# A channel mix contracted in two 64-deep halves instead of one 128-deep product

## The chip, the core and the metric

The kernel runs on one core of one Trainium2 chip. The metric is the device time of one execution in microseconds (us). A core has several engines with queues of their own: TensorE (PE; its weight loads are shown apart, as PEld) multiplies matrices into PSUM, VectorE (DVE), ScalarE (ACT) and GpSimd (POOL) work element by element, SyncE (SP) issues most of the transfers. Each engine works its queue in order; a semaphore makes an instruction wait for another engine.

## The reference

The input is x, 4 images of 64 channels of 256 by 256, in 32-bit floats. Four layers follow each other. Layers 0, 1 and 3 are long convolutions with a separable causal filter that a small network generates, each plus `x * bias`. Layer 2, which the change concerns, is a channel mix in the Haar domain with a soft threshold:

```python
f1 = haar2d(x)
acc = jnp.zeros_like(f1[:, :conv_w.shape[1]])
for i in range(v.shape[0]):                                   # two parts
    f3 = f1 * v[i]
    f4 = jnp.einsum('bchw,oc->bohw', f3, conv_w[i])
    f5 = jnp.sign(f4) * jax.nn.relu(jnp.abs(f4) - tau[i])
    acc = acc + f5
y = haar2d(acc, inverse=True)
return y + x
```

v and tau hold one value for each coefficient and part, the same for all channels; conv_w is 2 matrices of 64 by 64.

## The kernel before

The filters are made once, in the first 55 us, and written to DRAM. Then the four images are worked one after the other, each in three phases.

Phase A runs over the 64 channels. A convolution is two products with triangular matrices (lines 139 and 140), the data being the stationary operand; two convolutions are followed by a Haar transform down the columns (L197), and ScalarE copies the result into two large SBUF tiles z, one for each half of the columns, laid out as partition, row, channel. Phase C runs over the channels again: the inverse Haar transform (L286, L297), the residual, and the last convolution.

Phase B lies between them, runs over 64 groups of four rows of coefficients, and transfers nothing. A group is worked in two steps. `b_rows`: TensorE transforms along the rows (L227, product pg; two rows of 64 channels fill the 128 columns of a stationary operand, so the result has row r of the pair and channel c on partition 64 r + c), ScalarE copies it to f (L235), and three small VectorE operations of two elements mend the border coefficients (L238, L239, L240). `b_mix`: TensorE contracts the channels (L248, product px), VectorE scales by v (L258), ScalarE takes Abs into mag (L262) and Sign in place (L263), GpSimd subtracts tau (L264), VectorE clamps at 0 and multiplies by the sign (L265), and two GpSimd additions, one for each half of the columns, sum the two parts into z (L268).

Line 248 contracts 128 partitions although a row has 64 channels: the moving operand wb holds the mixing matrix twice, for row 0 in its upper 64 rows and first 128 columns, for row 1 in its lower 64 rows and last 128 columns, and zeros elsewhere. So one product of 256 columns gives both rows:

```python
wb = const.tile([P, 2, P], F32, name="wb")
nc.vector.memset(wb, 0.0)
for r in range(2):
    nc.sync.dma_start(wb[r * C : (r + 1) * C, r, :], wmix)
```

A product of 32-bit floats is carried out as two matmul instructions, each with a weight load of its own.

The order on the engines' queues is not that of the program text. The framework schedules the instructions by their dependencies and by its own estimate of their durations, so a changed instruction can move others on every engine. Pools set how far it can run ahead: f has 3 buffers, f4 and mag 2 each, px 2 (of two PSUM banks), pg and the other products 4. VectorE's butterfly on rows 0 and 128 of z stands before and after phase B.

Of the kernel before, what the change touches and what calls it, by code (L numbers as in the profile page):

```python
# [9 lines left out]
F32 = mybir.dt.float32  # L10
AF = mybir.ActivationFunctionType
ALU = mybir.AluOpType
PSUM = bass.MemoryType.PSUM
DRAM = bass.MemoryType.DRAM

B, C, S, EMB, ORD = 4, 64, 256, 33, 64
P = 128
# [1 line left out]

INV_2PI = float(np.float32(1.0 / (2.0 * math.pi)))  # L20
MAGIC = float(1.5 * 2.0**23)
# 2 pi in three parts, of which the first two give exact products with small integers
C1 = 6.28125
C2 = 2028.0 / 2.0**20
C3 = float(np.float32(2.0 * math.pi - C1 - C2))
# [6 lines left out]

@with_exitstack
def conv_seq_kernel(ctx, tc, x, fz, fw, bias, decay, haar, haar_inv, vt, taut, wmix, out):
    """Three separable causal long convolutions with a Haar-domain channel mix between the second and the third.

    The 2-D FFT convolution with k = hx (x) hy on a doubled grid is Tx X Ty^T / 512 with lower triangular
    Toeplitz Tx, Ty. A product with the data as the stationary operand contracts its partition axis and swaps
    the axes, so two of them give back the layout they started from. The filters are kept from the last value to
    the first: their Toeplitz matrices are then overlapping rows in DRAM, read back to front by the products.  # L40

    A Haar transform of 256 points is two local ones of 128 points whose sums are then added and subtracted;
    coefficients are kept in that order (block, local index), in which v and tau are laid out too.
    """
    nc = tc.nc

    const = ctx.enter_context(tc.tile_pool(name="const", bufs=1))
    dram = ctx.enter_context(tc.tile_pool(name="dram", bufs=1, space=DRAM))

# [1 line left out]
    hbt = const.tile([P, P], F32, name="hbt")  # L51
    hb = const.tile([P, P], F32, name="hb")
    hinv = const.tile([P, 2, S], F32, name="hinv")
    nc.sync.dma_start(hbt, haar[0])
    nc.sync.dma_start(hb, haar[1])
    nc.sync.dma_start(hinv, haar_inv)
    wb = const.tile([P, 2, P], F32, name="wb")
    nc.vector.memset(wb, 0.0)
    for r in range(2):
        nc.sync.dma_start(wb[r * C : (r + 1) * C, r, :], wmix)  # L60
    vsb = const.tile([P, S // 4, 16], F32, name="vsb")
    tsb = const.tile([P, S // 4, 16], F32, name="tsb")
    nc.scalar.dma_start(vsb, vt)
# [1 line left out]
    bsb = const.tile([P, 3, C], F32, name="bsb")  # L65
    nc.sync.dma_start(bsb, ap(bias, 0, [[0, P], [C, 3], [1, C]]))

# [1 line left out]
    pads = [dram.tile([C, 2, ROW], F32, name=f"pad{layer}") for layer in range(3)]  # L69
    with tc.tile_pool(name="filt", bufs=2) as fp, tc.tile_pool(name="fps", bufs=4, space=PSUM) as fps:  # L70
        dsb = fp.tile([C, S], F32, name="dsb", bufs=1)
        nc.sync.dma_start(dsb, decay)
        zs, ws = [], []
        for layer in range(3):
            z = fp.tile([EMB, S + 2 * ORD], F32, name=f"z{layer}", tag="z", bufs=3)
            nc.sync.dma_start(z, fz[layer])
            w = fp.tile([ORD, 2, 3 * ORD + 4], F32, name=f"w{layer}", tag="w", bufs=3)
            nc.sync.dma_start(w, fw[layer])
            zs.append(z)
            ws.append(w)  # L80
        cur = {}
        both = [(layer, axis) for layer in range(3) for axis in range(2)]
        for step in range(3):
            for layer, axis in both:
                z, w = zs[layer], ws[layer]
                ps = fps.tile([ORD, S], F32, name=f"fp{step}_{layer}_{axis}", tag="fps")
                if step == 0:
                    nc.tensor.matmul(ps, z[:, S + axis * ORD : S + (axis + 1) * ORD], z[:, :S], start=True, stop=True)
                else:
                    nc.tensor.matmul(  # L90
                        ps, w[:, axis, (step - 1) * ORD : step * ORD], cur[layer, axis], start=True, stop=True
                    )
                par = 3 * ORD
                u = fp.tile([ORD, S], F32, name=f"u{step}_{layer}_{axis}", tag="u", bufs=3)
                nc.vector.tensor_scalar(
                    u, ps, w[:, axis, par + step : par + step + 1], w[:, axis, par + 3 : par + 4], ALU.add, ALU.mult
                )
                # into [-pi, pi], where the Sin table is defined
                k = fp.tile([ORD, S], F32, name=f"k{step}_{layer}_{axis}", tag="k", bufs=3)
                nc.vector.tensor_scalar(k, u, INV_2PI, MAGIC, ALU.mult, ALU.add)  # L100
                nc.vector.tensor_scalar(k, k, -MAGIC, None, ALU.add)
                for c in (C1, C2, C3):
                    nc.vector.scalar_tensor_tensor(u, k, -c, u, ALU.mult, ALU.add)
                nc.vector.tensor_scalar(u, u, PI_IN, -PI_IN, ALU.min, ALU.max)
                h = fp.tile([ORD, S], F32, name=f"h{step}_{layer}_{axis}", tag="h", bufs=12)
                nc.scalar.activation(h, u, AF.Sin)
                cur[layer, axis] = h
        for layer, axis in both:
            w = ws[layer]
            ps = fps.tile([C, S], F32, name=f"fo_{layer}_{axis}", tag="fps")  # L110
            nc.tensor.matmul(ps, w[:, axis, 2 * ORD : 3 * ORD], cur[layer, axis], start=True, stop=True)
            f = fp.tile([C, ROW], F32, name=f"f_{layer}_{axis}", tag="f")
            nc.vector.memset(f[:, S:], 0.0)
            nc.vector.scalar_tensor_tensor(  # L114
                f[:, :S], ps, 1.0 / (2 * S) if axis == 0 else 1.0, dsb, ALU.mult, ALU.mult
            )
            nc.sync.dma_start(pads[layer][:, axis, :], f)

# [1 line left out]
    zpool = ctx.enter_context(tc.tile_pool(name="zpool", bufs=1))  # L120
    tp = ctx.enter_context(tc.tile_pool(name="toep", bufs=7))
    io = ctx.enter_context(tc.tile_pool(name="io", bufs=3))
# [2 lines left out]
    psx = ctx.enter_context(tc.tile_pool(name="psx", bufs=2, space=PSUM))  # L125

    def toeplitz(layer, c, name):
        """[p, k, m] = h_k[S - 1 - m - p], 0 where that is negative, for the filters down (0) and along (1)"""
        t = tp.tile([P, 2, S], F32, name=name, tag="toep")
        nc.sync.dma_start(t, ap(pads[layer], c * 2 * ROW, [[1, P], [ROW, 2], [1, S]]))  # L130
        return t
# [2 lines left out]
        return psm.tile([P, 2, S], F32, name=name, tag="mm")  # L134

    def contract(ps, src, t):
        """ps[:, m, :] = (the m-th half of src's free axis) x (causal filter of src's partition axis)"""
        for m in range(2):
            nc.tensor.matmul(ps[:, m, :], src[:, 0, m * P : (m + 1) * P], t[:, ::-1], start=True, stop=False)  # L139
            nc.tensor.matmul(ps[:, m, P:], src[:, 1, m * P : (m + 1) * P], t[:, : P - 1 : -1], start=False, stop=True)  # L140
# [5 lines left out]
                    stages[s](tick - s)  # L146

    def butterfly(z):
        """rows 0 and P of z: their sum and their difference"""
        d = mx.tile([P, C], F32, name="bfly", tag="bfly")  # L150
        nc.vector.tensor_sub(d, z[:, 0, :], z[:, P, :])
        nc.vector.tensor_add(z[:, 0, :], z[:, 0, :], z[:, P, :])
# [2 lines left out]
    for b in range(B):  # L155
        keep = dram.tile([C, P, 2, S], F32, name=f"keep{b}")
        z = [zpool.tile([P, S, C], F32, name=f"z{h}_{b}", tag=f"z{h}") for h in range(2)]

# [1 line left out]
        st = {}  # L160

        def a_load(c):
# [53 lines left out]
        for h in range(2):  # L216
            butterfly(z[h])

# [1 line left out]
        mixed = {}  # L220

        def b_rows(g):
# [19 lines left out]

        def b_mix(g):
            f = mixed.pop(g)
            ps = psx.tile([P, 2, 2, S], F32, name=f"px_{b}_{g}", tag="mix")
            for q in range(2):
                for h in range(2):
                    nc.tensor.matmul(  # L248
                        ps[:, h, q, :],
                        f[:, q, h * P : (h + 1) * P],  # L250
                        wb.rearrange("p r n -> p (r n)"),
                        start=True,
                        stop=True,
                    )
            scale = vsb[:, g, :].unsqueeze(2).to_broadcast([P, 16, C])
            shrink = tsb[:, g, :].unsqueeze(2).to_broadcast([P, 16, C])
            f4 = mx.tile([P, 16, C], F32, name=f"f4_{b}_{g}", tag="f4")
            nc.vector.tensor_tensor(  # L258
                f4, ps.rearrange("p h q (r i o) -> p (h q r i) o", r=2, i=2), scale, ALU.mult
            )  # L260
            mag = mx.tile([P, 16, C], F32, name=f"mag_{b}_{g}", tag="mag")
            nc.scalar.activation(mag, f4, AF.Abs)  # L262
            nc.scalar.activation(f4, f4, AF.Sign)  # L263
            nc.gpsimd.tensor_tensor(mag, mag, shrink, ALU.subtract)  # L264
            nc.vector.scalar_tensor_tensor(mag, mag, 0.0, f4, ALU.max, ALU.mult)  # L265
            parts = mag.rearrange("p (h r i) o -> p h r i o", h=2, i=2)
            for h in range(2):
                nc.gpsimd.tensor_tensor(  # L268
                    z[h][:, 4 * g : 4 * g + 4, :], parts[:, h, :, 0, :], parts[:, h, :, 1, :], ALU.add
                )  # L270

        pipelined(S // 4, [b_rows, b_mix])
        for h in range(2):
            butterfly(z[h])

# [1 line left out]
        def c_load(c):  # L277
            r = io.tile([P, 2, S], F32, name=f"r_{b}_{c}", tag="in", bufs=4)
            nc.sync.dma_start(r, keep[c])
# [36 lines left out]


def _haar_order():
    """the place in the reference's order of the coefficient (block, local index)"""
    at = np.zeros((2, P), np.int64)  # L320
    for q in range(2):
        at[q, 0] = q
        n = 1
# [4 lines left out]


def _haar_local():  # L330
    """rows: the 128-point Haar functions, the constant one divided by sqrt(2)"""
    h = np.zeros((P, P))
    h[0] = 1.0 / 16.0
    n = 1
# [76 lines left out]
```

## Time and profile before

| What | us |
|---|---|
| Median of 3 runs (4255.77 to 4256.11) | 4256.06 |
| Span of the profiled execution | 4252.5 |
| TensorE products px, L248, 2048 instructions | 598.1 |
| TensorE products pg, L227, 2048 instructions | 291.8 |
| GpSimd subtractions, L264, 256 of 2.002 | 512.0 |
| GpSimd additions, L268, 512 of 0.946 | 471.9 |
| VectorE clamp and multiply, L265, 256 of 1.634 | 418.2 |
| VectorE scale, L258, 256 of 1.216 | 310.7 |
| VectorE small operations, L238 to L240, 768 | 400.0 |
| ScalarE Abs and Sign, L262 and L263, 512 | 541.1 |

The span runs from the first to the last instruction of the profiled execution; the median is of whole executions and stands 3.6 us above it. Busy times of groups on the same engine overlap where instructions are pipelined, on TensorE above all, so they can't simply be added there. In a line of instructions the columns are the line of the kernel, the engine, the operation, what is written and read, and the shapes; "128*128" ahead of a shape gives rows and columns of the stationary operand. In a timeline the first two columns are the start and the duration, "x2" says that two instructions were merged into one line, and the brackets give idle time before it and what ended it. Where a line or tile is asked for by itself, its durations stand as least, median and greatest in ns, and the list below gives idle microseconds and how many times.

### The profile page before, as it was taken

What the parts mean: (1) busy time and instruction counts of PE and PEld (TensorE: products, weight loads), DVE (VectorE), ACT (ScalarE), POOL (GpSimd) and SP (SyncE); (2) the same over time, 40 slices, a digit from 0 to 9 for tenths busy, and PEclk for the clock granted to TensorE, in tenths of its full rate; (3) what the DMA queues carried; (4) which work ended last, traced back from release to release, by engine and by line L of the source; (5) the groups of instructions that cost most, each with busy time, mean ns of one, the idle gap of its engine ahead of it and who ended that gap; (6) DMA issues with size and microseconds to landing.
All of it is one profiled execution on the core that took longest, in us unless ns stands there. A gap on an engine that the chain in (4) does not pass through costs nothing.

```text
span 4252.5 us, 56979 instructions
## 1 busy us (share of the span) xinstructions
PE 3805.2 (89%) x21552; PEld 3445.5 (81%) x21552; DVE 1864.7 (44%) x2491; ACT 1531.2 (36%) x2323; POOL 975.2 (23%) x772
## 2 busy tenths in 40 slices
PE   7999876899999977699999997769999999676999
PEld 5999655799999965589999995559999998555998
DVE  4222788322222288822222228972222223886222
ACT  2333555222233355522233335542223333554222
POOL 0000588100000068800000007870000000776000
PEclk9999989899999998899999999889999999988999
DMA  4566100355555600045556650005555665000554
GB/s 127 171 172 173 45 1 1 109 149 152 164 171 172 173 21 1 1 131 150 151 168 172 172 169 1 1 3 149 151 150 170 172 173 144 1 1 22 152 151 124
DMA packets 424114, 476.23 MB, mean 112 GB/s; under 512 B 28993, under 2 KB 357924, under 8 KB 423844
## 3 DMA queue, kind: packets, MB, share of 16 engines
q1 hardware_dynamic: 317060, 337.29, 29.7%
q10 hardware_dynamic: 106784, 135.30, 8.7%
q8 instruction: 174, 2.85, 0.3%
q14 instruction: 96, 0.79, 0.1%
HBM read 337.67 MB, written 134.81 MB: 111 GB/s over the span
## 4 chain that ended last, share of the span: by engine, by line
PE 72%; POOL 11%; DVE 10%; issue 4%; ACT 3%; DMA 0%; SPq 0%; POOLq 0%; DVEq 0%; ACTq 0%
PE py L139 16%; PE pa L139 16%; PE pw L286 11%; PE pa L140 8%; PE py L140 8%; POOL mag L264 6%; PE pz L197 5%; PE pu L297 5%; POOL z L268 5%; DVE mag L265 5%; PE px L248 2%; DVE f L258 2%; ACT mag L262 1%; PE pg L227 1%; DVE f L239 1%
## 5 line engine op out<-in xcount | busy, mean ns | idle before, releaser
L264 POOL TENSOR_TENSOR mag<-mag,tsb 128x1024 f32<-128x1024 f32 x256 | 512.0, 2002 | 2856.4 <-ACT mag L262 2775.4
L173 ACT COPY a<-pa 128x512 f32<-128x512 f32 x768 | 450.3, 586 | 1470.7 <-PE pa L140 1470.7
L139 PE MATMUL py<-t,a 128*128 128x256 f32 x3072 | 918.5, 381 | 5.9 <-ACT a L173 5.9
L248 PE MATMUL px<-wb,f 128*128 128x256 f32 x2048 | 598.1, 438 | 363.2 <-DVE f L239 147.9
L248 PEld LDWEIGHTS px<-wb,f 128*128 128x128 f32 x2048 | 412.9, 216 | 492.3 <-issue 133.7
L140 PEld LDWEIGHTS py<-t,a 128*128 128x128 f32 x3072 | 583.7, 190 | 78.9
L140 PE MATMUL py<-t,a 128*128 128x128 f32 x3072 | 590.1, 274 | 0.0
L286 PE MATMUL pw<-hinv,z 128*128 128x256 f32 x2048 | 502.0, 388 | 33.1 <-POOL z L268 33.1
L286 PEld LDWEIGHTS pw<-hinv,z 128*128 128x128 f32 x2048 | 474.9, 302 | 46.0 <-POOL z L268 36.6
L139 PEld LDWEIGHTS py<-t,a 128*128 128x128 f32 x3072 | 486.3, 192 | 15.3 <-ACT a L173 8.8
L186 DVE SCALAR_TENSOR_TENSOR y<-y,bsb,py 128x512 f32<-128x512 f32 x256 | 191.5, 748 | 699.8 <-PE py L140 695.0
L268 POOL TENSOR_TENSOR z<-mag 128x256 f32<-128x256 f32 x512 | 471.9, 946 | 77.0 <-DVE mag L265 30.5
L265 DVE SCALAR_TENSOR_TENSOR mag<-mag,f 128x1024 f32<-128x1024 f32 x256 | 418.2, 1634 | 144.2 <-POOL mag L264 141.1
L186 DVE SCALAR_TENSOR_TENSOR y<-u,bsb,py 128x512 f32<-128x512 f32 x256 | 191.3, 747 | 604.2 <-PE py L140 594.7
L262 ACT ACTIVATE mag<-f 128x1024 f32<-128x1024 f32 x256 | 270.3, 1056 | 504.7 <-POOL z L268 313.5
L186 DVE SCALAR_TENSOR_TENSOR y<-x,bsb,py 128x512 f32<-128x512 f32 x256 | 191.3, 747 | 490.8 <-PE py L140 490.8
L299 DVE TENSOR_TENSOR u<-pu,r 128x512 f32<-128x512 f32 x256 | 177.1, 692 | 394.8 <-PE pu L297 394.8
L290 ACT COPY w<-pw 128x512 f32<-128x512 f32 x256 | 150.0, 586 | 547.5 <-PE pw L286 547.5
L258 DVE TENSOR_TENSOR f<-px,vsb 128x1024 f32<-128x1024 f32 x256 | 310.7, 1216 | 12.2 <-PE px L248 8.9
L139 PE MATMUL pa<-t,x 128*128 128x256 f32 x1024 | 306.9, 382 | 4.8 <-DVE f L114 4.8
L227 PEld LDWEIGHTS pg<-hbt,z 128*128 128x128 f32 x2048 | 292.2, 212 | 20.7 <-ACT z L201 6.0
L139 PE MATMUL pa<-t,y 128*128 128x256 f32 x1024 | 305.8, 380 | 0.0
(44 smaller groups left out, 4393.6 us busy)
## 6 DMA issues: line engine op xcount, KB each, us to landing
t<-pad SPq DMA_DIRECT2D x768, 256.0 KB, 3.5
x<-in_x SPq DMA_DIRECT2D x256, 256.0 KB, 3.7
keep<-y ACTq DMA_DIRECT2D x256, 256.0 KB, 3.3
r<-keep SPq DMA_DIRECT2D x256, 256.0 KB, 2.6
out_y<-y ACTq DMA_DIRECT2D x256, 256.0 KB, 3.3
pad<-f SPq DMA_DIRECT2D x6, 96.0 KB, 2.7
vsb<-in_vt ACTq DMA_DIRECT2D x1, 512.0 KB, 4.0
tsb<-in_taut ACTq DMA_DIRECT2D x1, 512.0 KB, 5.1
```

The lines of the kernel that those rows point to most:

```text
L139: nc.tensor.matmul(ps[:, m, :], src[:, 0, m * P : (m + 1) * P], t[:, ::-1], start=True, stop=False)
L140: nc.tensor.matmul(ps[:, m, P:], src[:, 1, m * P : (m + 1) * P], t[:, : P - 1 : -1], start=False, stop=True)
L173: nc.scalar.copy(a, ps)
L186: nc.vector.scalar_tensor_tensor(y, s[res], bsb[:, layer, c : c + 1], ps, ALU.mult, ALU.add)
L227: nc.tensor.matmul(ps[:, q, h * P : (h + 1) * P], z[h][:, r : r + 2, :].rearrange("p r c -> p (r c)"), hbt, start=True, stop=True,)
L248: nc.tensor.matmul(ps[:, h, q, :], f[:, q, h * P : (h + 1) * P], wb.rearrange("p r n -> p (r n)"), start=True, stop=True,)
L258: nc.vector.tensor_tensor(f4, ps.rearrange("p h q (r i o) -> p (h q r i) o", r=2, i=2), scale, ALU.mult)
L262: nc.scalar.activation(mag, f4, AF.Abs)
L264: nc.gpsimd.tensor_tensor(mag, mag, shrink, ALU.subtract)
L265: nc.vector.scalar_tensor_tensor(mag, mag, 0.0, f4, ALU.max, ALU.mult)
L268: nc.gpsimd.tensor_tensor(z[h][:, 4 * g : 4 * g + 4, :], parts[:, h, :, 0, :], parts[:, h, :, 1, :], ALU.add)
L286: nc.tensor.matmul(ps[:, m, :], z[h][:, m * P : (m + 1) * P, c], hinv[:, h, :], start=(h == 0), stop=(h == 1))
```

## The change

wb shrinks to one copy of the mixing matrix on each half of the partitions, without zeros. Each product of 128 partitions by 256 columns becomes two of 64 partitions by 128 columns, one for each row of the pair, whose operands lie on partitions 0 to 63 and 64 to 127. The row r becomes the outermost axis of px[...]. The axes that follow (those of v and tau, prepared on the host, and of mag in the additions) are reordered to match; the additions write rows 0, 2, 1, 3 of the group.

```diff
-    wb = const.tile([P, 2, P], F32, name="wb")
-    nc.vector.memset(wb, 0.0)
+    wb = const.tile([P, P], F32, name="wb")
     for r in range(2):
-        nc.sync.dma_start(wb[r * C : (r + 1) * C, r, :], wmix)
+        nc.sync.dma_start(wb[r * C : (r + 1) * C, :], wmix)
...
-            ps = psx.tile([P, 2, 2, S], F32, name=f"px_{b}_{g}", tag="mix")
-            for q in range(2):
-                for h in range(2):
-                    nc.tensor.matmul(
-                        ps[:, h, q, :],
-                        f[:, q, h * P : (h + 1) * P],
-                        wb.rearrange("p r n -> p (r n)"),
-                        start=True,
-                        stop=True,
-                    )
+            ps = psx.tile([P, 2, 2, 2, P], F32, name=f"px_{b}_{g}", tag="mix")
+            for h in range(2):
+                for q in range(2):
+                    for r in range(2):
+                        on = slice(r * C, (r + 1) * C)
+                        nc.tensor.matmul(
+                            ps[:, r, h, q, :], f[on, q, h * P : (h + 1) * P], wb[on, :], start=True, stop=True
+                        )
...
-                f4, ps.rearrange("p h q (r i o) -> p (h q r i) o", r=2, i=2), scale, ALU.mult
+                f4, ps.rearrange("p r h q (i o) -> p (r h q i) o", i=2), scale, ALU.mult
...
-            parts = mag.rearrange("p (h r i) o -> p h r i o", h=2, i=2)
+            parts = mag.rearrange("p (r h q i) o -> p r h q i o", r=2, h=2, q=2)
             for h in range(2):
                 nc.gpsimd.tensor_tensor(
-                    z[h][:, 4 * g : 4 * g + 4, :], parts[:, h, :, 0, :], parts[:, h, :, 1, :], ALU.add
+                    z[h][:, 4 * g : 4 * g + 4, :].rearrange("p (q r) o -> p r q o", q=2),
+                    parts[:, :, h, :, 0, :],
+                    parts[:, :, h, :, 1, :],
+                    ALU.add,
                 )
...
-        return lay(a.reshape(2, S // 4, 4, 2, P).transpose(4, 1, 3, 2, 0).reshape(P, S // 4, 16))
+        return lay(a.reshape(2, S // 4, 2, 2, 2, P).transpose(5, 1, 3, 4, 2, 0).reshape(P, S // 4, 16))
```

The rest of the diff drops comments, which shifts line numbers: in the changed kernel the product px is L251, the scale L257, Abs and Sign L261 and L262, the subtraction L263, the clamp L264 and the addition L267.

## The prediction

> **What bounds the kernel now.** I read the busy table first, then the granted clock and busy time in the four stretches of the channel mix, then who waits for the lines that the change touches, and last the timeline of GpSimd and VectorE inside one stretch.
>
> ```profile
> PE 3805.2 (89%) x21552; PEld 3445.5 (81%) x21552; DVE 1864.7 (44%) x2491; ACT 1531.2 (36%) x2323; POOL 975.2 (23%) x772
> ...
> 60.00:452.00 392.00, 389.98 (x2543) 363.53 (x2541) 95.88 (x131) 140.79 (x255) 0.00 (x0) 1.00 0.61 173
> 452.00:765.00 313.00, 214.53 (x1031) 176.90 (x1032) 266.49 (x330) 163.87 (x192) 245.27 (x192) 0.87 0.00 1
> ```
>
> Columns of the last two lines: stretch, length, busy time of PE, PEld, DVE, ACT, POOL, clock, DMA share, GB/s. TensorE's 89% is an average over different stages. Phase A of the first image (60 to 452) fills TensorE: 390 of 392 us. Phase B (452 to 765), the only stage that the change touches, has it busy for 215 of 313 us, while VectorE is busy for 266 and GpSimd for 245. The other three images' phase B are within 4 us of these figures. So in phase B TensorE is not the engine to relieve; who waits for its product says the same:
>
> ```profile
> L258 DVE TENSOR_TENSOR f<-px,vsb x256: 1208/1212/1226, 456.6 to 3901.7; 128x1024 f32<-128x1024 f32 x128
> ...
>   ACT f L235: 22.3, 14
>   DVE f L258: 8.9, 14
> ```
>
> The product px (L248) is read by L258. VectorE stood idle for it for 8.9 us in the whole run, and ScalarE's copies (L235), queued on TensorE behind it, for 22.3 us. The chain of waits gives px 2% (85 us), but that is where the chain happens to pass, not what would vanish.
>
> What does set phase B is seen in the spread of durations:
>
> ```profile
> L265 DVE SCALAR_TENSOR_TENSOR mag<-mag,f x256: 1210/1728/2949, 461.3 to 3906.1; 128x1024 f32<-128x1024 f32 x128
> ...
> L268 POOL TENSOR_TENSOR z<-mag x512: 712/733/1807, 464.2 to 3908.1; 128x256 f32<-128x256 f32 x171
> ...
>   ACT mag L262: 313.5, 121
> ```
>
> L258, with one input in PSUM, never varies (1208 to 1226 ns). L265, with both in SBUF, runs from 1210 to 2949, and GpSimd's L268 from 712 to 1807: they stand in each other's way. The last line (asked of L268) says that ScalarE's Abs (L262) waited 313.5 us for the additions L268 to free a mag buffer.
>
> GpSimd's timeline shows what this costs. First a piece where two subtractions (L264) follow each other, then a piece where L264 and the pair L268 alternate:
>
> ```profile
> 572.85 1.89 POOL L264 TENSOR_TENSOR mag<-mag,tsb 128x1024 f32<-128x1024 f32 x1
> 575.26 2.50 POOL L264 TENSOR_TENSOR mag<-mag,tsb 128x1024 f32<-128x1024 f32 x1 [0.52 <-ACT mag L262]
> 577.72 1.41 POOL L268 TENSOR_TENSOR z<-mag 128x256 f32<-128x256 f32 x2
> 580.30 1.90 POOL L264 TENSOR_TENSOR mag<-mag,tsb 128x1024 f32<-128x1024 f32 x1 [1.17 <-DVE f L239]
> 582.16 3.79 POOL L268 TENSOR_TENSOR z<-mag 128x256 f32<-128x256 f32 x4
> 585.92 1.89 POOL L264 TENSOR_TENSOR mag<-mag,tsb 128x1024 f32<-128x1024 f32 x1
> ...
> 529.33 1.90 POOL L264 TENSOR_TENSOR mag<-mag,tsb 128x1024 f32<-128x1024 f32 x1 [1.17 <-ACT mag L262]
> 531.19 2.40 POOL L268 TENSOR_TENSOR z<-mag 128x256 f32<-128x256 f32 x2
> 534.75 1.90 POOL L264 TENSOR_TENSOR mag<-mag,tsb 128x1024 f32<-128x1024 f32 x1 [1.17 <-ACT mag L262]
> ...
> 533.62 1.06 ACT L262 ACTIVATE mag<-f 128x1024 f32<-128x1024 f32 x1 [2.94 <-POOL z L268]
> ```
>
> The first piece does three groups in 585.92 - 572.85 = 13.07 us, 4.36 each. The second takes 534.75 - 529.33 = 5.42 us for one: after L268 the next subtraction waits for an Abs (1.06 us) that could only start when L268 freed the second of two mag buffers[...]. So the order in which GpSimd's queue was built prices phase B.
>
> [...]
>
> **The change, part by part.**
>
> Removed: per group four products of 256 columns, each as two passes, so 8 matmul instructions. Sixteen in a row took 3.69 us at 454.62; without the last one's 0.38 that is 0.22 us each, so 1.76 us per group. Added: eight 64-deep products of 128 columns, 16 instructions. L227, of the same columns but full depth, issues sixteen in 1.95 us at 458.15, 0.112 us apart once the last one's 0.275 is taken off. If the halves gain nothing, that is 16 x 0.112 = 1.79 us. If the two row halves overlap perfectly, 0.90. Two mode changes per group I bound by one pipeline depth each, 0.275 - 0.112 = 0.16 us, so up to 0.33. The new product costs between 0.90 and 2.12 us per group against 1.76; over 64 groups TensorE's 215 us become 160 to 238, still under the 313. I take 1.4 us and charge nothing: VectorE and GpSimd cover it. Only the first group of an image has no cover: L258 there waited 1.27 us for px. I take 0.4 us off per image, between a gain of 1.0 and a loss of 0.4: -1.6 us in all.
>
> L258 reads the same 1024 contiguous PSUM values: 0. The shorter wb and the memset gone (0.27 us at the start): 0; the filter loads queue on SP behind wb's, so at most 0.3 us is won. L268 keeps its count and size; its output is now written in rows 0, 2, 1, 3 and three dimensions instead of one run. No such form is in the trace. Its input was already in runs of 64, so I take 0, with -20 to +50 ns each; at 128 per image on the bounding path, -10 to +26 us in all.
>
> Moved: the scheduler orders the queues anew. In the built programs phases A and C keep their order on TensorE, ScalarE and SP; VectorE differs there by one copy of a butterfly. Phase B differs on all four compute queues, alike in the four images. I write for GpSimd how many groups' L268 stand after each L264 before the next one:
>
> ```
> before 0120121021020111111111201201201201201210111111111201201201201121
> after  0111210202102110111111120111120112020202101201111111201111201112
> ```
>
> I cut both into blocks: 0, some 1s, 2; or a lone 1. The times are the distances of L264's starts in the first image (459.02 to the end of the last L268 at 764.43, 305.4 us). Before: ten "012", of which the first two took 14.79 and 14.15 (filling up) and the others 13.21 on average; two "02" at 8.65 and 9.01 (8.83); four lone 1s, 5.26 on average; two with nine 1s, 56.5 and 56.7 (13.21 + 8 x 5.42 = 56.6, so each further 1 costs 5.42); one "0112", 18.9. After: six "02", 53.0; five lone 1s, 26.3; one "012", 13.2; one "0112", 18.6; two with three 1s, 2 x 24.05 = 48.1; two with four, 2 x 29.47 = 58.9; two with seven, 2 x 45.73 = 91.5. Sum 309.6, and 2.5 for filling up (1.58 + 0.94 above): 312.1. That is +6.7 us per image, +26.8 in four: 22 further 1s instead of 17 at 5.42 - 4.40 = 1.02 each are most of it, one more lone 1 the rest. VectorE's order inside the new blocks repeats that of the old ones (multiply, a small operation or two, scale of the group two ahead), which is why I carry the prices over.
>
> Sum against the profiled execution's own 4252.5 us: +26.8 - 1.6 = +25.2, so 4277.7. The median shown is 3.6 us above that span: 4281.
>
> **The rivals.**
>
> Faster: the shorter product is worth what the chain shows. TensorE's queue clears sooner, the ScalarE copies and L258 never wait, and the freed VectorE time fills the holes in the alternation. For it: 85 us of chain on px, 22.3 + 8.9 us of waits. Against it: L268, not px, ends Abs's waits in the alternation. It would give 4256 - 31 = 4225, at best 4256 - 43 (half the chain's share) = 4213.
>
> The same: the block prices don't carry over, since holes move to where another operation fills them: 4248 to 4265. For it, one lone 1 took only 4.70 us.
>
> Much slower, by TensorE: the halves don't overlap,[...] and px arrives late for L258. Before, 18 groups have at most one large VectorE operation between the edge copy (L240) that releases px and L258, and one such wait was already 0.28 us; after, 15 have. It decides once px takes some 1.5 us more than now, which the bound above excludes at full clock; but the clock in phase B is 0.87. Price 15 x 1.5 x 4 = 90 us on top: up to 4371, about 4330 if half of it is felt.
>
> Slower by GpSimd: the new L268 form takes 50 ns more: 4281 + 26 = 4307.
>
> **How the numbers follow.** Forecast with its own bounds (4262 to 4300): 0.54. Faster 0.15, same 0.12, slow TensorE 0.11, slow L268 0.08. A change under 0.2%, 8.5 us, can't be told from none. The same rival stays within that, the forecast and the two slow ones are beyond: faster 0.15, same 0.12, slower 0.73. The range 4238 to 4325 leaves out most of the faster rival and half of the slow TensorE one, together 0.17.
>
> **What would show it.** Right: 16 matmul instructions per group at L251 of the new kernel, TensorE's phase B time down with no shorter phase; the four stretches of phase B some 6 to 7 us longer; subtractions again 5.4 us apart in the runs of 1s, their wait ended by Abs. Wrong: a median of additions off 0.73 us, L258 waiting for px for tens of us, subtractions in the alternation at another spacing, or phases A and C changed by more than 2 us each. Should phase B be shorter although the runs of 1s keep 5.42, the lone 1s and "02" blocks are what I mispriced.

## The result, and the profile after

| | before | after |
|---|---|---|
| Median of 4 runs each on one chip | 4256.09 | 4283.17 |
| Span of the profiled execution | 4252.5 | 4282.3 |
| Start of phase B: first pg to first subtraction, mean of the images | 6.97 | 6.19 |
| Blocks of phase B: first subtraction to last addition, mean of the images | 305.5 | 313.3 |
| Mean TensorE clock over the span | 0.962 | 0.919 |

The ratio is 1.0063, with a 95% interval of 1.0048 to 1.0077: the change makes the kernel slower by 27 us. The two spans differ by 29.8 us. Of these, 31.2 are the blocks of the four phases B, -3.1 their starts, and 2.9 the first phase A (455.0 us against 452.1). This last part doesn't go with the change: executions with the old product below have 452.0 to 455.0 us, those with the new one 451.9 to 455.0. The rest, -1.2 us, lies between the phases B and at the end.

The busy table of the changed kernel's page, and from its costliest groups the two of TensorE in phase B (columns: instructions, busy time, mean ns of one, idle time before them):

```profile
PE 3779.8 (88%) x23600; PEld 3447.8 (81%) x23600; DVE 1865.6 (44%) x2490; ACT 1528.3 (36%) x2323; POOL 983.7 (23%) x772
...
L251 PE MATMUL px<-wb,f 64*128 64x128 f32 x4096 | 439.1, 363 | 386.2 <-DVE f L257 144.7
...
L227 PE MATMUL pg<-hbt,z 128*128 128x128 f32 x2048 | 401.8, 355 | 10.3 <-ACT f L235 4.9
```

px fell from 598.1 to 439.1 us. But pg, which nobody touched, rose from 291.8 to 401.8. The same two stretches of the first image as before, in the same columns:

```profile
60.00:452.00 392.00, 391.73 (x2540) 364.93 (x2539) 95.07 (x128) 139.66 (x253) 0.00 (x0) 1.00 0.60 172
452.00:772.00 320.00, 208.12 (x1548) 178.03 (x1548) 268.02 (x333) 164.40 (x194) 244.45 (x190) 0.73 0.01 3
```

Phase A is as it was. Phase B's granted clock is 0.73 where it was 0.87, so TensorE is busy for 208 us, hardly less than the 215 before, although the products px are half as deep; VectorE and GpSimd have the same work (268 and 244 us) in a longer stretch. Who waits for px, asked of the tile:

```profile
L257 DVE TENSOR_TENSOR f<-px,vsb x256: 1207/1212/1227, 458.7 to 3926.5; 128x1024 f32<-128x1024 f32 x128
...
  ACT f L235: 40.9, 29
...
  DVE f L257: 1.9, 4
```

The scale waits 1.9 us for it in the whole run (8.9 before), though ScalarE's copies, queued on TensorE behind px, wait 40.9 (22.3 before). And what the additions do, asked of their line:

```profile
L267 POOL TENSOR_TENSOR z<-mag x512: 715/738/1733, 466.3 to 3938.5; 128x256 f32<-128x256 f32 x171
...
  ACT mag L261: 331.8, 120
```

A median of 738 ns against 733: the new form of the addition costs some 5 ns. ScalarE's Abs waited 331.8 us for these additions to free a mag buffer (313.5 before). The timeline of GpSimd and ScalarE inside a run of 1s is the old one:

```profile
546.47 1.90 POOL L263 TENSOR_TENSOR mag<-mag,tsb 128x1024 f32<-128x1024 f32 x1 [1.17 <-ACT mag L261]
548.33 2.39 POOL L267 TENSOR_TENSOR z<-mag 128x256 f32<-128x256 f32 x2
551.89 1.90 POOL L263 TENSOR_TENSOR mag<-mag,tsb 128x1024 f32<-128x1024 f32 x1 [1.17 <-ACT mag L261]
...
550.75 1.06 ACT L261 ACTIVATE mag<-f 128x1024 f32<-128x1024 f32 x1 [2.80 <-POOL z L267]
```

551.89 - 546.47 = 5.42 us for a group, as before, and the kernel now has more such groups. Cut into the prediction's blocks, an image takes: the two with three 1s 25.18 and 24.14; the two with four 29.64 and 29.62; the two with seven 46.16 and 46.13; "0112" 18.68; "012" 13.21; the five lone 1s 24.6 together; the six "02" 55.9. That is 313.3 us.

### The profile page after: what moved, and what is told of

It is laid out like the page before. It is cut to its first block, busy times and chain, and to the rows that moved or that the text cites. A ratio compares the mean times of both kernels' runs of the same rounds, so it can differ in the third digit from the quotient of the medians.

```text
span 4282.3 us, 61138 instructions
## 1 busy us (share of the span) xinstructions
PE 3779.8 (88%) x23600; PEld 3447.8 (81%) x23600; DVE 1865.6 (44%) x2490; ACT 1528.3 (36%) x2323; POOL 983.7 (23%) x772
## 4 chain that ended last, share of the span: by engine, by line
PE 69%; POOL 12%; DVE 11%; issue 5%; ACT 1%; DMA 0%; POOLq 0%; SPq 0%; DVEq 0%; ACTq 0%
PE py L139 16%; PE pa L139 16%; PE pw L288 11%; PE pa L140 8%; PE py L140 8%; POOL mag L263 7%; POOL z L267 6%; DVE mag L264 6%; PE pz L197 5%; PE pu L299 5%; DVE f L257 2%; DVE f L239 1%; DVE fd L238 1%; ACT mag L261 1%; PE px L251 0%
## 5 line engine op out<-in xcount | busy, mean ns | idle before, releaser
L263 POOL TENSOR_TENSOR mag<-mag,tsb 128x1024 f32<-128x1024 f32 x256 | 502.3, 1967 | 2856.7 <-ACT mag L261 2811.3
L251 PE MATMUL px<-wb,f 64*128 64x128 f32 x4096 | 439.1, 363 | 386.2 <-DVE f L257 144.7
L251 PEld LDWEIGHTS px<-wb,f 64*128 64x128 f32 x4096 | 360.4, 252 | 457.8 <-issue 231.3
L267 POOL TENSOR_TENSOR z<-mag 128x256 f32<-128x256 f32 x512 | 489.4, 981 | 98.7 <-DVE fd L238 33.6
L264 DVE SCALAR_TENSOR_TENSOR mag<-mag,f 128x1024 f32<-128x1024 f32 x256 | 430.4, 1684 | 173.8 <-POOL mag L263 173.1
L139 PEld LDWEIGHTS py<-t,a 128*128 128x128 f32 x3072 | 486.7, 192 | 15.3 <-ACT a L173 8.8
L261 ACT ACTIVATE mag<-f 128x1024 f32<-128x1024 f32 x256 | 269.8, 1055 | 510.6 <-POOL z L267 331.8
L227 PE MATMUL pg<-hbt,z 128*128 128x128 f32 x2048 | 401.8, 355 | 10.3 <-ACT f L235 4.9
L227 PEld LDWEIGHTS pg<-hbt,z 128*128 128x128 f32 x2048 | 340.8, 251 | 56.0 <-issue 28.6
L257 DVE TENSOR_TENSOR f<-px,vsb 128x1024 f32<-128x1024 f32 x256 | 309.2, 1217 | 6.3 <-PE px L251 1.9
```

Of the source, the lines that this page charges most:

```text
L227: nc.tensor.matmul(ps[:, q, h * P : (h + 1) * P], z[h][:, r : r + 2, :].rearrange("p r c -> p (r c)"), hbt, start=True, stop=True,)
L251: nc.tensor.matmul(ps[:, r, h, q, :], f[on, q, h * P : (h + 1) * P], wb[on, :], start=True, stop=True)
L257: nc.vector.tensor_tensor(f4, ps.rearrange("p r h q (i o) -> p (r h q i) o", i=2), scale, ALU.mult)
L267: nc.gpsimd.tensor_tensor(z[h][:, 4 * g : 4 * g + 4, :].rearrange("p (q r) o -> p r q o", q=2), parts[:, :, h, :, 0, :], parts[:, :, h, :, ...
```

## The experiments

Besides the two kernels, twelve were run. The ratio is to runs of the kernel before made beside each of them, whose medians lie between 4255.57 and 4258.62 us. In the table, phase B is its start plus its blocks, the mean of the four images of the profiled execution; the clock is the mean over that execution.

| Kernel | Product px | Order of the queues | mag buffers | Median, us | Ratio to before, 95% interval | Phase B, us | Clock |
|---|---|---|---|---|---|---|---|
| before | 128 deep | its own | 2 | 4256.09 | 1 | 312.5 | 0.962 |
| after | 64 deep | its own | 2 | 4283.17 | 1.0048 to 1.0077 | 319.5 | 0.919 |
| new_mm_old_order | 64 deep | before's, TensorE left free | 2 | 4272.70 | 1.0027 to 1.0057 | 316.9 | 0.910 |
| old_mm_new_order | 128 deep | after's, TensorE left free | 2 | 4302.28 | 1.0095 to 1.0125 | 323.3 | 0.957 |
| new_mm_all_old | 64 deep | before's | 2 | 4262.34 | 1.0001 to 1.0018 | 313.4 | 0.915 |
| old_mm_all_new | 128 deep | after's | 2 | 4318.23 | 1.0127 to 1.0161 | 328.0 | 0.956 |
| full_depth | eight of 128 deep | after's | 2 | 4294.37 | 1.0075 to 1.0109 | 321.8 | 0.956 |
| after_mag3 | 64 deep | the scheduler's; after's but on TensorE | 3 | 4186.79 | 0.9823 to 0.9853 | 295.6 | 0.925 |
| before_mag3 | 128 deep | the scheduler's | 3 | 4183.15 | 0.9812 to 0.9841 | 293.9 | 0.970 |
| after_triples | 64 deep | "012" throughout, TensorE left free | 2 | 4202.72 | 0.9857 to 0.9886 | 299.2 | 0.913 |
| triples_mag3 | 64 deep | "012" throughout, TensorE left free | 3 | 4193.35 | 0.9835 to 0.9864 | 297.0 | 0.919 |
| triples_all | 64 deep | "012" throughout | 2 | 4160.37 | 0.9757 to 0.9789 | 289.1 | 0.932 |
| triples_all_mag3 | 64 deep | "012" throughout | 3 | 4154.12 | 0.9744 to 0.9773 | 287.0 | 0.930 |
| old_mm_triples_all | 128 deep | "012" throughout | 2 | 4159.04 | 0.9752 to 0.9785 | 287.8 | 0.964 |

An order is held like this: b_rows and b_mix note each instruction by its kind and group, and edges that only fix the order of issue, without a semaphore, chain the instructions of phase B on each engine in a written order. These lines shift the line numbers of the kernels that have them.

```diff
+ORDER = {
+    "DVE": "d0 lo0 hi0 d1 lo1 hi1 sc0 sc1 d2 lo2 hi2 mul0 d3 sc2 mul1 lo3",
...
+    "POOL": "sub0 sub1 zadd0 sub2 zadd1 zadd2 sub3 sub4 zadd3 sub5",
...
+def keep_order(tc, made):
+    for names in ORDER.values():
+        chain = [i for n in names.split() for i in made[n]]
+        for one, two in zip(chain, chain[1:]):
+            tc.add_manual_dep(
+                two,
+                one.name,
+                mybir.DependencyInfo(mybir.DependencyClass.NoSync, mybir.DependencyReason.DATA),
+                reason="order",
+            )
...
-            nc.gpsimd.tensor_tensor(mag, mag, shrink, ALU.subtract)
+            note("sub", g, nc.gpsimd.tensor_tensor(mag, mag, shrink, ALU.subtract))
```

The theory: the loss is the new order of the queues, and the product itself hardly counts. The rivals: the product's new form costs time by itself (the changes between 64-deep and 128-deep products, which the prediction calls mode changes; the lower clock), or the faster product was worth something that the order took back.

### The new product in the old order, and the old one in the new

new_mm_old_order is the changed kernel with the order of before on VectorE, ScalarE and GpSimd; old_mm_new_order is the kernel before with the order of after on these three.

> The changed kernel, with VectorE, ScalarE and GpSimd held in phase B to the order that they had before the change. If the order is the whole cost (theory), the subtractions fall into the old blocks, 305 us an image, and the shorter start of an image, 6.2 us instead of 7.0, stays: 4256 - 3 = 4253 us, between 4246 and 4261. If the 64-deep products cost the time, through TensorE's lower clock or its mode changes (first rival), or the new form of the additions does (second rival), it stays at 4283 +- 6.

> The kernel before, with VectorE, ScalarE and GpSimd held in phase B to the order that they have after the change. Theory: 313 us an image and the old start of 7.0 us, so 4283 + 3 = 4286 us, between 4278 and 4294. Both rivals: 4256 +- 6, since neither the 64-deep products nor the new additions are in it.

Both missed: they came out 20 and 16 us slower than the theory said, and outside its ranges. The first stands 10 us below the changed kernel and the second 46 above the kernel before, so the rivals' figures (4283 and 4256) are missed too. TensorE's queue, left to the scheduler, now put px ahead of pg: in new_mm_old_order ScalarE's copies waited 93.7 us for pg (42.9 before), and blocks "012" that took 13.1 to 13.4 before took up to 16.85. So three held queues are not the old order, and the comparison was made again with TensorE held too:

```diff
+    "PE": "pg0*1 pg1*1 pg0*3 pg1*3 pg2*2 px0*8 px1*8 pg2*2 pg3*4 pg4*2 px2*8",
...
+                        note("px", g, px)
```

> The changed kernel with TensorE's queue held to the old order as well, so that all four compute queues stand in phase B as before the change. If the queues' order is what costs (theory), the 17 us that the run with three held queues kept come from TensorE's own order, which was left free there and put products ahead of ones that ScalarE waits for: 4253 us, between 4246 and 4261. If the 64-deep products cost time themselves (rival), about 4270 stays.

> The kernel before with all four compute queues held in phase B to the order after the change. Theory: 313 us an image and a start of 7.0 us, plus some 2 us an image for the slower product as in the full-depth run: 4286 to 4294 us. Rival (the 64-deep products are the cost): 4256 +- 6. If the old product itself doesn't fit that order, 4302 as with three held queues.

new_mm_all_old gave 4262.34, 1.3 us above the theory's upper end and 8 below the rival's 4270: with the queues back in their old order, some 21 of the 27 us are gone. The changes between the two depths, the lower clock and the new additions are all in this kernel, so what they cost, less what the shorter product gains, is at most the 6 us that are left. The starts are 0.8 us shorter, as in the changed kernel, and every block has its old price within 0.6 us but one. It is a "012" at 624.57, and it takes 15.53 us where the kernel before took 13.43. Its timeline, GpSimd and then VectorE:

```profile
624.57 1.93 POOL L347 TENSOR_TENSOR mag<-mag,tsb 128x1024 f32<-128x1024 f32 x1
629.05 1.90 POOL L347 TENSOR_TENSOR mag<-mag,tsb 128x1024 f32<-128x1024 f32 x1 [2.54 <-DVE f L325]
...
624.66 1.90 DVE L233 COPY z<-bfly 128x64 f32<-128x64 f32 x1
626.61 1.21 DVE L343 TENSOR_TENSOR f<-px,vsb 128x1024 f32<-128x1024 f32 x1
```

A copy of VectorE's butterfly (L233), which the held chains don't contain, started 0.09 us after a subtraction of GpSimd and took 1.90 us instead of the 0.18 that the first such copy took, at 630.40, in the kernel before; the scale L343, its Abs and the next subtraction are late by that. The blocks of an image are 1.7 us longer than before (307.2 against 305.5), the starts 0.8 shorter; four times the difference is 3.6 us, and the spans differ by 3.3 (4255.8 against 4252.5). The profiled execution was the fastest of twelve, 4.7 us under their median, so this accounts for half of the 6 us; the rest isn't seen in the trace. In the old order the new product thus gains 3 us at the starts, and no gain shows in the blocks.

old_mm_all_new was a miss: 24 us above the upper end of the theory, and 16 above the 4302 foreseen for the case that the old product doesn't fit that order. Who waited for its px, asked of the tile:

```profile
  ACT f L320: 103.8, 49
...
  DVE f L344: 19.1, 24
```

and a stretch of its timeline, TensorE and GpSimd:

```profile
473.01 5.68 PE L333 MATMUL px<-wb,f 128*128 128x256 f32 x20
...
477.42 1.90 POOL L348 TENSOR_TENSOR mag<-mag,tsb 128x1024 f32<-128x1024 f32 x1 [4.74 <-ACT mag L346]
```

Twenty instructions take 5.68 us, 0.28 each, where sixteen took 3.69 (0.22 each) at the full clock. The granted clock was 0.50 from 469 to 475.3 us; the first five of the twenty are 0.43 us apart, those from the seventh on 0.22. The scale comes late, and the subtraction stands 4.74 us. (In full_depth, the next experiment, the same group's subtraction stands 2.57 us, and the clock there is 1.00.) In this order the old product does make others wait.

### The new order with products of full depth

full_depth is the changed kernel with its eight products of 128 columns, contracted over all 128 partitions with the half-zero wb. It computes the same, and all four queues are in exactly the order of after. Only the depth differs, and with it the chance of overlap.

```diff
-    wb = const.tile([P, P], F32, name="wb")
+    wb = const.tile([P, 2, P], F32, name="wb")
+    nc.vector.memset(wb, 0.0)
...
-                            ps[:, r, h, q, :], f[on, q, h * P : (h + 1) * P], wb[on, :], start=True, stop=True
+                            ps[:, r, h, q, :], f[:, q, h * P : (h + 1) * P], wb[:, r, :], start=True, stop=True
```

> The changed kernel with all 128 rows contracted against a half-zero wb, eight products of 128 columns a group: the queues of all engines are in the same order as after the change, only the two row halves no longer overlap. TensorE's px goes from about 1.0 to 1.8 us a group. Theory: nobody but the first group of an image waits for px, 4283 + 3 = 4286 us, between 4279 and 4296. If px is on the path of every group, 0.8 us x 256 = 205 us more, 4488; even a fifth of it is over 4320.

It took 4294.37 us, in the theory's range but 8 us above its figure. Half the depth is worth 11 us in the order of after: of the 9.8 between the spans 3.4 are at the starts (four times 7.05 less 6.19) and 5.6 in the blocks (four times 314.75 less 313.34), so it isn't only the first group of an image that waits for px: ScalarE's copies wait 63.8 us for it in the whole run, 40.9 in after. From its page, the groups of the same two products, in the columns as above:

```profile
L251 PE MATMUL px<-wb,f 128*128 128x128 f32 x4096 | 618.0, 309 | 350.3 <-DVE f L257 127.1
...
L228 PE MATMUL pg<-hbt,z 128*128 128x128 f32 x2048 | 307.0, 298 | 12.6 <-ACT f L236 7.3
```

Half the depth takes 179 us off px (618.0 to 439.1) and puts 95 on pg (307.0 to 401.8). Two things do that. The first is the change between 64-deep and 128-deep products, which full_depth doesn't have: where pg follows px, its second instruction comes 0.213 us after the first (the median at the full clock; 0.112 in full_depth). With 264 runs of pg that makes some 34 us of the 95. The rest, some 60 us, goes with the clock. The same 280 us of the first phase B, first in full_depth, then in after:

```profile
456.00:736.00 280.00, 199.88 (x1415) 190.30 (x1414) 238.64 (x294) 146.59 (x173) 213.42 (x169) 0.87 0.00 1
```

```profile
456.00:736.00 280.00, 190.72 (x1438) 163.82 (x1436) 239.62 (x300) 147.48 (x175) 214.56 (x168) 0.74 0.00 1
```

With nearly as many instructions in the same order, the granted clock is 0.87 with 128-deep products and 0.74 with 64-deep ones. In the records the clock is either 1.00 or 0.50: over the four phases B TensorE stood at the half clock for 27% of the time in full_depth and for 53% in after, and pg's instructions inside a run are 0.112 us apart at the one and 0.213 at the other.

### A third mag buffer

If the alternation costs 5.42 us because the next Abs has to wait for the addition that frees one of two mag buffers, a third buffer must take the wait away at the same order.

```diff
-            mag = mx.tile([P, 16, C], F32, name=f"mag_{b}_{g}", tag="mag")
+            mag = mx.tile([P, 16, C], F32, name=f"mag_{b}_{g}", tag="mag", bufs=3)
```

> The changed kernel with three mag buffers instead of two; VectorE, ScalarE and GpSimd keep the order of the changed kernel. Theory: in the runs of 1s Abs no longer waits for the additions, so each of the 22 further 1s of an image loses the 1.02 us by which 5.42 stands above 4.40: 4283 - 4 x 22.4 = 4193 us, between 4180 and 4225. [...]

It took 4186.79 us. GpSimd's timeline in the run of 1s that was shown above:

```profile
546.84 1.92 POOL L263 TENSOR_TENSOR mag<-mag,tsb 128x1024 f32<-128x1024 f32 x1 [1.07 <-ACT mag L261]
548.73 2.42 POOL L267 TENSOR_TENSOR z<-mag 128x256 f32<-128x256 f32 x2
551.10 1.91 POOL L263 TENSOR_TENSOR mag<-mag,tsb 128x1024 f32<-128x1024 f32 x1
```

551.10 - 546.84 = 4.26 us a group instead of 5.42, and the idle time ahead of the next subtraction is gone. What ScalarE's Abs waited for the additions, 331.8 us before, is gone as well (asked of L267):

```profile
  ACT mag L261: 1.3, 1
```

The blocks with seven 1s fall from 46.1 to 39.9 us, "02" and the lone 1s stay. VectorE, ScalarE and GpSimd kept their order, TensorE's was moved in places. The wait for the second buffer is the cause of the alternation's price.

before_mag3 is the same edit of the kernel before, with whatever order the scheduler makes of it.

> The kernel before with three mag buffers and the order that the scheduler gives it then. If the change's cost is the holes of the alternation (theory), the difference between the two kernels shrinks once a third buffer fills them: the shorter product then gives its 0.8 us at the start of an image and little else, so 4187 + 4 to 4187 + 14, 4191 to 4201 us. If the 64-deep product itself costs some 25 us (rival), the kernel before stays ahead: about 4160.

It took 4183.15 us, 8 us less than the theory's lower end and 3.6 less than after_mag3; the two intervals overlap. Both explanations missed here: nothing is left of the change's cost, and no gain shows either. Each of the two kernels has its own order, so this compares the change together with the order that comes with it.

### A good order, written out

The block "012" costs 4.36 us a group even with two buffers. So all of phase B was held to a repeated "012"; in triples_all and triples_all_mag3 TensorE too, in after_triples and triples_mag3 only the other three.

```diff
+        "sub0 sub1 zadd0 zadd1 sub2 sub3 zadd2 sub4 zadd3 zadd4 sub5 sub6 zadd5 sub7 zadd6 zadd7 sub8 sub9 "
...
+        "pg0 pg1 pg2 px0 pg3 px1 px2 pg4 pg5 px3 pg6 px4 px5 pg7 pg8 px6 pg9 px7 px8 pg10 pg11 px9 pg12 px10 "
```

> The changed kernel with VectorE, ScalarE and GpSimd held to the pattern of the old 012 blocks throughout, two mag buffers as before. Theory: 64 groups at 4.36 to 4.40 us and some 4 us of start and end, 284 us an image instead of 313.3: 4283 - 118 = 4165 us, between 4150 and 4190. [...]

> The same pattern with three mag buffers. Theory: the pattern leaves no hole for the third buffer to fill, so it equals the run before it within 10 us. If buffers still hold it back, it is faster by more than 20 us.

after_triples missed, 38 us above its figure and 13 above its range: three blocks of an image took 16.2 to 17.4 us, the others 13.1. Ahead of the first the scheduler had put 36 instructions of pg in a row on TensorE, those of four and a half groups:

```profile
499.21 5.42 PE L289 MATMUL pg<-hbt,z 128*128 128x128 f32 x36
```

The subtraction behind them, at 502.09, had stood idle for 4.33 us. The second of the three holds the butterfly. triples_mag3 was 9.4 us faster, within what was expected.

> The changed kernel in the repeated 012 pattern with TensorE's queue held to it too (one product px, one pg, two px, two pg). In the run without that, three blocks of an image took 16.3 to 17.4 us instead of 13.1, two of them where TensorE had been given several pg products ahead of a px and worked them at a low clock. Theory: those two go, the third (where VectorE's butterfly falls in) stays: 4203 - 4 x 7.4 = 4173 us, between 4160 and 4185. If a low clock makes TensorE late wherever it stands, 4203 +- 9.

> The same with three mag buffers. Theory: nothing waits for mag in this pattern, within 10 us of the run before it. If lateness elsewhere is soaked up by the third buffer, it is faster by 10 us or more.

triples_all took 4160.37 us, as the theory of blocks said at its lower end. GpSimd's timeline:

```profile
483.91 1.89 POOL L340 TENSOR_TENSOR mag<-mag,tsb 128x1024 f32<-128x1024 f32 x1
486.32 2.50 POOL L340 TENSOR_TENSOR mag<-mag,tsb 128x1024 f32<-128x1024 f32 x1 [0.52 <-ACT mag L338]
...
491.37 1.90 POOL L340 TENSOR_TENSOR mag<-mag,tsb 128x1024 f32<-128x1024 f32 x1 [1.17 <-DVE f L317]
...
496.98 1.91 POOL L340 TENSOR_TENSOR mag<-mag,tsb 128x1024 f32<-128x1024 f32 x1
```

496.98 - 483.91 = 13.07 us for three groups, nearly all through the image: a block with the butterfly takes 15.3 to 15.6, its neighbour 13.6. triples_all_mag3 was 6.3 us faster, within what was expected; at 4154.12 it has the lowest median of all, 2.4% under the kernel before.

Last, old_mm_triples_all has the product of the kernel before in this order.

> The product of the kernel before (128 rows deep, 256 columns, half-zero wb), with all four queues held in the repeated 012 pattern of triples_all, mag in two buffers. It tells whether the half-depth product is worth anything in an order that has no blocks of alternation. Theory (no one waits for px in the middle of phase B; the half-depth product only shortens the start of an image, 0.85 us on each of four): 4160 + 3.4 = 4164, with up to 20 us more if the two groups of every image whose ScalarE copies waited for pg at a low clock wait longer for the slower px: 4164 to 4184. Rival (the slower product doesn't fit an order that gives px little time, as in old_mm_all_new, where the copies waited for px 104 us): above 4200.

It took 4159.04 us, 5 us below the theory's lower end and 1.3 less than triples_all, so the two can't be told apart. The first phase B of old_mm_triples_all, then of triples_all:

```profile
456.00:736.00 280.00, 210.23 (x1022) 173.91 (x1020) 257.08 (x325) 163.39 (x192) 235.24 (x188) 0.88 0.00 1
```

```profile
456.00:736.00 280.00, 190.91 (x1534) 167.97 (x1532) 258.14 (x324) 161.41 (x190) 235.36 (x187) 0.77 0.00 1
```

TensorE is busy for 210 us with the old product and 191 with the new; VectorE and GpSimd get through the same work either way. The starts are 0.44 us shorter with the new product, and its block with the butterfly costs 2 us more (15.3 to 15.6, where such a block takes 13.1 with the old one). In an order without alternation the change is worth nothing.

## Why the prediction was right

The forecast was 4281 us, slower; 4283.17 was measured. By its steps:

- **TensorE isn't what phase B waits for**: right. The scale's wait for px fell to 1.9 us and phase B grew. The faster rival, which counted on these waits, fell; in the good order the shorter product brings nothing. ScalarE's copies do wait more for it, though (40.9 us against 22.3), and full_depth shows that in the order of after a slower product is felt.
- **The cost of px**: forecast between 0.90 and 2.12 us a group, with 1.4 taken. TensorE's timeline at the start of phase B, the two products one after the other:

```profile
457.53 2.06 PE L251 MATMUL px<-wb,f 64*128 64x128 f32 x32
459.52 2.05 PE L227 MATMUL pg<-hbt,z 128*128 128x128 f32 x16
```

  32 instructions of px in 2.06 us are (2.06 - 0.275) / 31 = 0.058 us apart, so 0.92 us a group; those of full depth are 0.112 apart. Inside a run of px the two row halves overlap almost fully (0.058 against 0.056, half of 0.112). A change from 64-deep to 128-deep products shows too: the last px starts at 457.53 + 2.06 - 0.275 = 459.32 and the first pg 0.20 us later, and the sixteen of pg take 2.05 us where they took 1.95 before. Over the whole run, at the full clock, the first two steps of pg behind px take 0.202 and 0.213 us at the median; in full_depth both take 0.112. One such change costs 0.19 us, a little more than the prediction's bound of 0.16. The way back into px can't be read as cleanly, since waits for f fall there. With one change each way for a group, px costs at least 0.92 + 0.19 = 1.1 us at the full clock: inside the bounds.
- **The clock**: left as it was in the forecast, which had TensorE's phase B at 160 to 238 us. It fell from 0.87 to 0.73, and 208 us were measured. That was left out and did little harm, since TensorE had time to spare (208 of 320 us).
- **The start of an image**: forecast -0.4 us, measured -0.78. The first px of an image runs at the full clock (1.00 in all four), where it saves 0.84 us a group (1.76 less 0.92).
- **The additions' new form**: forecast 0, measured 5 ns at the median; the rival of 50 ns fell.
- **The order of the queues**: the step that carries the sum. Forecast 312.1 us of blocks an image, measured 313.3. The blocks with seven 1s were forecast at 45.73 and took 46.15, those with four 29.47 and 29.63; the block with three 1s that comes first took 25.18, less than its 24.05 with the 2.5 for filling up. "02" was forecast at 8.83 and took 9.32 in the mean (one of 10.76 holds the butterfly): +2.9 us an image. The lone 1s were forecast at 5.26 and took 4.92: -1.7. These are terms of the sum that were mis-sized, and they nearly cancel. The prediction's count of "22 further 1s instead of 17" takes the block "0112" in on one side only (it is 23 and 17); the sum of the blocks doesn't rest on it.
- **Median above span**: 3.6 us was carried over, 0.9 measured. Together with the longer first phase A (2.9 us) it happens to come out even: span against span the forecast was 4.6 us short (4277.7 against 4282.3), and the 2 us between the medians are partly luck. Phases A and C changing by more than 2 us each were named as a sign of being wrong; only the first phase A did, and, as said of the spans above, not with the change.

That the order is the cause was only argued in the prediction; new_mm_all_old shows it for some 21 of the 27 us; of the 6 that are left, half is one butterfly copy less the starts' gain, and half isn't explained. The argument that the product is free wherever VectorE and GpSimd are the bound held in the old order and in the good one. In the order of after it holds only for the faster product: full_depth loses 11 us to the changed kernel and old_mm_all_new 35. Why the latter loses 24 more than full_depth is only in part known: in the piece shown TensorE works px at half the clock, where full_depth has the full clock. What brings it there stays open. Its second product of four already needs the border copy that the first four of eight don't need, and its products are longer; the two weren't separated.

## What to carry to other kernels

Where a scheduler builds the queues from its own estimate of durations, a change to one instruction is a change of every queue; compare the built orders and price what they do to the resource that is short before counting the cycles saved. A hole that opens because a buffer comes free late is mended by a third buffer or by a written order (1.6% and 2.3% here, 2.4% together), and only then can one see what a faster instruction is worth, which in the written order was nothing. When testing an order, hold every queue that takes part, down to the small operations: TensorE's left free cost 10, 39 and 42 us in three pairs and saved 16 in a fourth, and one loose copy cost 2 us an image.

## What the runs showed of the hardware

- The 64-deep products lower the granted clock of TensorE in phase B (456 to 736 us), in each pair of the same order: 0.74 against 0.87 (after, full_depth), 0.77 against 0.88 (triples_all, old_mm_triples_all) and 0.72 against 0.89 (new_mm_all_old, before). Busy time as the trace counts it doesn't sort these runs: TensorE was busy for 196.8 us of the 280 at 0.72 (new_mm_all_old) and for 195.4 at 0.87 (old_mm_all_new). What it is about the 64-deep products that lowers the clock was not tried. More than half of px's gain of 179 us (95, after against full_depth) went back into a slower pg, by the clock and by the changes from 64-deep to 128-deep products.
- A change from 64-deep to 128-deep products costs 0.19 us at the full clock (0.202 and 0.213 us for two steps in after that take 0.112 each in full_depth).
- A VectorE copy of 64 elements a partition takes 0.19 us at 452.05 in the kernel before, where GpSimd is idle, and 1.90 in new_mm_all_old, where it starts 0.09 us after a GpSimd subtraction: nearly as long as that subtraction itself (1.93). The three edge operations of two elements, 0.15 us at least, go up to 1.9 in the same way: in the kernel before, the 155 of 768 that overlap no GpSimd instruction take 0.146 to 0.172 us, and all 340 that take more than 0.4 overlap one (L238 at 482.79 took 1.49 us, to 484.28; a subtraction ran from 482.36 to 484.26). One of the three, in the kernel before:

```profile
L240 DVE COPY f<-fd x256: 150/661/1942, 454.5 to 3896.3; 128x2 f32<-128x2 f32 x128
```

  The clamps show the same: the 21 of 256 (L265) that overlap no GpSimd instruction take 1.21 to 1.23 us, the others up to 2.95. The scales (L258) take 1.21 to 1.23 us, although 252 of 256 overlap one. The prediction tells these two apart by where their inputs lie, one in PSUM or both in SBUF. The butterfly's copy and L240 have a single input, in SBUF, and vary as well (0.18 to 1.90 and 0.15 to 1.94 us); what tells them apart from L258 was not tried.
